# Attention blocks of four tokens, 64 moving columns instead of 128, with two buffers for keys and values

## The chip, the cores and the metric

The kernel runs on one NeuronCore of a Trainium2 chip, with float32 data throughout. The metric is the device time of one execution in microseconds (us). Five engines are named as in the profile: PE (matrix products, with PEld for its weight loads), DVE (vector), ACT (scalar and activation), POOL (GpSimd), and SP, which here does nothing but issue transfers. Transfers run on 16 DMA engines that all queues share.

## The reference, cut to what matters

There are 64 sequences of 64 tokens with 256 features. Four layers follow one another, each added to its input: a conditioned low-rank layer (0), a layer whose weights are decoded from the condition (1), an attention (2) and a set of normalised tables with a two-layer network (3). The change lies in layer 2, whose attention is unusual: it does not go over tokens. Within each token the 256 features are 16 heads of 16 numbers, and the heads attend to one another. Queries, keys and values are the same array:

```python
kx = modulated_linear(x, s, k_aff_w, k_aff_b, k_w, k_b)
kx = kx.reshape(B, N, H, D)          # H = D = 16
q = k = v = kx
scores = jnp.einsum('bnhd,bnjd->bnhj', q, k) / math.sqrt(D)
A = jax.nn.softmax(scores, axis=-1)
out = jnp.einsum('bnhj,bnjd->bnhd', A, v).reshape(B, N, F)
out = modulated_linear(out, s, o_aff_w, o_aff_b, o_w, o_b)
```

So every one of the 4096 tokens has two products of 16x16 by 16x16.

## The kernel before

**Tiling.** Layers 0, 1 and the first half of layer 2 (`layers01`) work on chunks of 512 tokens, eight in all. Attention (`fetch` and `attention`) and the rest (`layers23`) work on 16 pieces `P` of 256 tokens.

**Attention as block products.** PE contracts over 128 partitions, but a token needs only 16. The kernel puts 8 tokens (digit `b`, 8 x 16 = 128 partitions) on the partitions, and for each of 32 groups `g` of eight tokens runs one product with 128 moving columns. The moving side is block-diagonal: `kb` holds the keys of token `b` only in columns of block `b`, with zeros elsewhere, so that the eight tokens do not mix. The weight side has 32 columns, and four groups go to the four 32-column strips of the array, by the partitions of their output. A group has 16 heads as weight columns, so 16 of its 32 weight columns are zeros: `kz` holds the heads of each group between zeros, and two groups `h` = 0 and 1 add into one strip (`start=(h == 0), stop=(h == 1)`). This is L789 (`pS`), 32 products a piece, which the profile counts as 64 matmul records, two for each float32 product. L813 (`pv`) does the same with the softmax weights `at_` against the block-diagonal values `vb`, into two PSUM banks, again 32 products a piece.

**How the operands get there.** ACT writes the keys of layer 2 to `kT` (L710), PE transposes them (`pt`, L721), ACT copies them to `kk` (L727, L730). SP writes `kk` to DRAM as `kd` (L736, two transfers in 64-byte runs) and `vd` (L744, four transfers in 64-byte runs). `fetch` reads them back: `kc` (L754, one transfer), which ACT copies between the zeros of `kz` (L756); eight transfers into the blocks of `kb` (L762); eight into the blocks of `vb` (L767). There are two `kz` tiles, used in turn, and one `kb` and one `vb`, both inside the tile `kv`. After the scores DVE and ACT make the softmax (L796 to L801), DVE transposes it to `at_` (L803), PE runs L813, ACT copies both banks to `av` (L818), SP writes `av` to DRAM as `ad` (L822, 512 KB) and reads it back turned as `aT` (L829, two transfers in 256-byte runs). `layers23` then begins with `aS` (L877) and the output projection `po` (L883, L886).

**What sets the order.** Nothing is issued as written. Each piece of work is a `step` with an engine, an estimated cost, what it reads and writes and a rank. `Plan.order` lists them greedily: on each engine the step that can start first by the plan's own estimates, ties by rank, goes next. The ranks are shifted by the tables `LEAD` (by stage) and `SHIFT` (by stage and piece), and `SLACK` says how much later a step of better rank may start and still be preferred. The result is one fixed sequence per engine, and each engine waits in it in order. SP's sequence holds nearly all transfers.

Of the kernel before, what the change touches and what calls it, by code (L numbers as in the profile page):

```python
# [61 lines left out]
class Plan:  # L62
# [3 lines left out]
    LANES, ISSUE, LAND, HOP, SLACK = 8, 0.54, 2.3, 0.12, 0.0  # L66
    TABLE = 1.4

    LEAD = {"down": 946.4, "fetch": 1090.6, "gather": 1168.5, "hidden": 1056.4, "keys": 938.1, "last": 1046.3,
            "load": 934.3, "load W1": 1568.6, "load W2": 1287.4, "load decoder": 1245.0, "load first": 604.2, "load ids": 902.1,  # L70
            "load keys": 911.3, "load states": 1260.1, "load up": 753.0, "mid": 546.9, "norm": 984.7, "out": 1165.7,
            "park": 927.1, "scores": 1120.2, "set W1": 1041.3, "set decoder": 215.9, "set down": 150.6, "set k": 952.6,
            "set o": 868.6, "set states": 1178.6, "turn": 1040.2, "up": 1091.5, "values": -313.8}


    SHIFT = {"down": (121.0, 0.0, -136.0, 0.0, 45.3, 0.0, 57.2, 0.0, 669.8, 0.0, 452.8, 0.0, 448.6, 0.0, 203.0, 0.0),
            "fetch": (-21.2, -95.4, 22.4, 39.5, 73.9, 129.8, -198.4, 143.2, 60.9, 236.7, -128.9, -10.1, -60.7, 22.7, -201.3, -74.5),
            "gather": (25.1, 20.6, -52.3, 44.9, 149.5, 295.4, 273.6, -73.2, 25.2, 4.2, 71.4, 347.0, 156.9, 181.1, 284.4, 233.7),
            "hidden": (-23.7, -102.8, 100.9, 97.4, -70.1, 56.9, 93.3, -244.5, -119.8, 73.4, -11.9, 193.5, 100.1, -16.4, -8.7, 2.5),
            "keys": (-138.5, 0.0, -157.5, 0.0, 320.2, 0.0, 194.1, 0.0, 169.5, 0.0, 259.2, 0.0, 207.7, 0.0, 209.6, 0.0),  # L80
            "last": (-49.6, -146.3, 100.1, 60.6, -162.7, -187.0, 32.8, 25.1, 68.0, -10.7, 96.6, -194.4, -61.8, 407.3, 397.6, 375.4),
            "load": (0.0, 0.0, 0.0, 0.0, 311.2, 0.0, 24.7, 0.0, -364.5, 0.0, 23.9, 0.0, 66.9, 0.0, 299.3, 0.0),
            "mid": (-25.3, 0.0, -351.6, 0.0, -179.2, 0.0, -1.1, 0.0, -6.1, 0.0, 131.7, 0.0, 213.3, 0.0, 249.5, 0.0),
            "norm": (-246.5, -272.7, -139.3, -283.8, -207.2, -15.7, -104.9, 40.1, -219.1, 16.5, -133.9, -101.4, -119.9, 129.5, 13.2, -265.9),
            "out": (75.9, 13.0, -112.7, -113.3, -174.2, 11.1, 82.9, 26.4, 125.1, -118.1, 220.2, -0.8, 136.4, 254.8, -8.3, 195.2),
            "park": (-302.5, 0.0, -53.5, 0.0, -775.7, 0.0, -547.9, 0.0, -550.1, 0.0, -359.8, 0.0, -152.5, 0.0, 238.3, 0.0),
            "scores": (-82.8, 70.4, 67.7, -137.7, -106.8, -38.2, 26.9, 83.3, 98.4, 82.9, 84.9, -0.6, 136.4, 144.2, 34.2, 171.0),
            "turn": (-82.0, 10.3, -20.8, -18.4, -23.5, -0.8, 77.8, 214.9, 84.7, 115.0, -41.3, 77.4, -122.1, 45.8, 69.3, 164.8),
            "up": (-344.7, 0.0, -102.1, 0.0, -238.6, 0.0, -224.7, 0.0, -115.4, 0.0, -84.9, 0.0, -54.9, 0.0, -53.0, 0.0),
            "values": (-74.2, 53.7, -70.1, -159.6, 81.8, 307.5, -59.3, -54.8, 80.6, -145.4, -166.2, -196.3, -101.8, -85.7, -218.8, 125.5)}  # L90
# [12 lines left out]
    @staticmethod  # L103
    def keys(things):
        out = []
        for t in things:
            if isinstance(t, tuple) and isinstance(t[0], Buf):
                out.append((t[0], t[1]))
            else:
                out.append((t, None))  # L110
        return out
# [147 lines left out]
def tile_kernel(ctx: ExitStack, tc: tile.TileContext, a: dict, out: bass.AP):  # L259
# [15 lines left out]
    BUFS = {"x": 3, "xr": 3, "pw": 2, "cg": 2, "mg": 2, "ei": 2, "oh": 2, "t4": 3, "kk": 2, "kc": 1, "act": 2, "E": 2,  # L275
# [5 lines left out]
    def bank(name, tag="B"):  # L281
        return Buf(ps, tag, {"A": 2, "B": 3, "C": 2, "S": 1}[tag], [128, 512], name, turns=(tag == "A"))
# [35 lines left out]

    styleq = fixed("styleq", [128, 2, B // PB, 4, 2])
# [14 lines left out]
    kz = [fixed(f"kz{i}", [128, 32 * NG + 16]) for i in range(2)]  # L334

    kv = fixed("kv", [128, 2 * NG * 128])
    kb, vb = (kv[:, i * NG * 128 : (i + 1) * NG * 128].rearrange("p (b g j) -> p b g j", g=NG, b=8) for i in range(2))
    at_ = fixed("at", [128, 32 * NH + 16])


    def consts():
# [4 lines left out]
    step("POOL", 0.4, lambda: (nc.gpsimd.memset(neghalf, -0.5), nc.gpsimd.memset(V, 0.0), nc.gpsimd.memset(bigtab, 0.0),  # L346
                               nc.gpsimd.memset(at_[:, 32 * NH :], 0.0)),
         w=["neghalf", "V", "at0", "zeros"], rank=-107)
# [138 lines left out]
    for n, half in (("kb", 0), ("vb", 1)):  # L487
        step("POOL", 3.5, lambda half=half: nc.gpsimd.memset(kv[:, half * NG * 128 : (half + 1) * NG * 128], 0.0),
             w=[n] + [f"W_dec{i}" for i in range(NW)], rank=-104)


    for n in "ko":
# [8 lines left out]
        if n == "o":  # L501
            step("DVE", 1.0, lambda: [nc.vector.tensor_copy(
                styleq[:, k].rearrange("p c (q z) l -> p c q z l", z=2)[:, :, :, z, :], style["o"][:, k, :].rearrange("p (c l q) -> p c q l", l=2, q=2))
                for k in range(2) for z in range(2)], r=["style_o"], w=["styleq"], rank=rk)
# [117 lines left out]
    kds, vds, kcs, xds = {}, {}, {}, {}  # L622

    def layers01(c, rank):
# [66 lines left out]
        for h in range(2):  # L691
# [11 lines left out]
             r=X + ["style_k"], w=[xs], rank=rank)  # L703
        kT = sb("t4", [128, 2, CH], f"kT_{c}")
        pk = banks(f"pk_{c}")
        for o in range(2):
# [3 lines left out]
                nc.scalar.activation(kT()[:, o, b * S : (b + 1) * S], pk[o]()[:, b * S : (b + 1) * S], AF.Identity,  # L710
                                     scale=demod["k"][:, o, b0 + b : b0 + b + 1], bias=col["k_b"][:, o : o + 1])
                for b in range(CB)], r=[pk[o], "demod_k", "cols"], w=[(kT, o)], rank=rank)
        for p in range(2):
# [19 lines left out]
            kd = kds[P] = Buf(dram, "kd", 2 * NC, [HD, PT, NH], f"kd_{P}")  # L733
            vd = vds[P] = Buf(dram, "vd", 2 * NC, [8, NH, NG, HD], f"vd_{P}")
            for t in range(2):
                step("SP", 0.75, lambda t=t, kk=kk, kd=kd: nc.sync.dma_start(  # L736
                    kd()[:, t * 128 : (t + 1) * 128, :].rearrange("d p h -> p d h"),
                    kk()[:, 0, t, :].rearrange("p (d h) -> p d h", h=NH)), r=[(kk, t)], w=[(kd, t)], rank=rank + PERIOD * p, dma=(131072, 64), late=1.5)
            for cc in range(4):
                def f(cc=cc, kk=kk, vd=vd):  # L740
                    k = kk()
                    src = k[cc : cc + 1, 1]
                    src = bass.AP(src.tensor, src.offset, [[4 * k.ap[0][0], 32], [HD, 2 * NH], [1, HD]])
                    nc.sync.dma_start(vd()[2 * cc : 2 * cc + 2].rearrange("l h g d -> g (l h) d"), src)  # L744
                step("SP", 0.78, f, r=[(kk, 2)], w=[(vd, cc)], rank=rank + PERIOD * p, dma=(65536, 64), late=1.5)

    def fetch(P, rank):


        plan.stage = "fetch"  # L750
        kd, vd = kds[P], vds[P]

        kc = kcs[P] = sb("kc", [128, NG * NH], f"kc_{P}")
        step("SP", Plan.ISSUE, lambda: nc.sync.dma_start(kc(), kd().rearrange("d (b g) h -> (d b) (g h)", b=8)), r=[kd], w=[kc], rank=rank, dma=(262144, 2048))  # L754
        z = P % 2
        step("ACT", act(512), lambda: nc.scalar.copy(view(kz[z], [[32, NG], [1, NH]], 16), kc().rearrange("p (g h) -> p g h", h=NH)),  # L756
             r=[kc], w=[f"kz{z}"], rank=rank)
        for b in range(8):

            def f(b=b):  # L760
                dst = kb[b : b + 1, (b % 4) * 2 + b // 4]
                nc.sync.dma_start(bass.AP(dst.tensor, dst.offset, [[8 * dst.ap[0][0], HD], [1, NG * NH]]),  # L762
                                  kd()[:, b * NG : (b + 1) * NG, :].rearrange("d g h -> d (g h)"))
            step("SP", 0.63, f, r=[kd, "kb"], w=[f"kb.{b}"], rank=rank, dma=(32768, 2048))
        for b in range(8):

            step("SP", 0.50, lambda b=b: nc.sync.dma_start(  # L767
                vb[b * 16 : (b + 1) * 16, b].rearrange("p g d -> p (g d)"), vd()[b].rearrange("h g d -> h (g d)")),
                r=[vd, "vb"], w=[f"vb.{b}"], rank=rank, dma=(32768, 2048))

    def parts(n):
        return [f"{n}.{b}" for b in range(8)]

    aTs = {}

    def attention(P, rank):

        kzt = kz[P % 2]
        fetch(P, rank)
        plan.stage = "scores"  # L780

        pS = bank(f"pS_{P}", "S")

        def f():
            for r in range(4):
                for h in range(2):
                    for cc in range(4):
                        g = h * 16 + r * 4 + cc
# [258 lines left out]
```

## Time and profile before

| | |
|---|---|
| median of 9 runs | 487.79 us (481.22 to 494.13) |
| the profiled execution's own time | 491.37 us |
| its span, first to last instruction | 489.6 us |
| PE busy | 423.6 us (87%) |
| DVE, ACT, POOL busy | 308.7, 297.0, 155.3 us |
| mean granted TensorE clock | 0.923 |
| DMA | 192668 packets, 83.53 MB; the SP queue's packets took 50.8% of 16 engines' span |

Busy time of an engine counts the time in which at least one of its instructions ran; matmuls on different strips run side by side, so the mean of one instruction times their number is more than the busy time. The chain that ended last follows the work back from the last instruction, at each step to what released it. It is one path through an execution: taking time off it shows what can be won, and another path may then be the longer one. A DMA-issuing instruction on SP lasts as long as SP is held up by it, and counts as issue (SPq), not as busy.

### The profile page before, as it was taken

How to read it: one execution, taken by the hardware profiler on the slowest of the kernel's cores; microseconds unless marked ns; L12 is line 12 of the kernel's file. 1: busy time of each engine (PE TensorE's matmuls, PEld its weight loads, DVE VectorE, ACT ScalarE, POOL GpSimd, SP SyncE). 2: the span in 40 equal slices, each digit the busy share in tenths (PEclk: the TensorE clock that was granted, in tenths of full speed). 3: DMA queues.
4: the chain of work that ended last, by engine and by line, in shares of the span. 5: the costliest groups of instructions: out<-in, count | busy, mean ns of one | idle time of the engine just before them, and what ended most of it. 6: DMA issues, size and time to landing. Idle time of an engine off the chain costs nothing.

```text
span 489.6 us, 11060 instructions
## 1 busy us (share of the span) xinstructions
PE 423.6 (87%) x4026; PEld 321.7 (66%) x4026; DVE 308.7 (63%) x668; ACT 297.0 (61%) x875; POOL 155.3 (32%) x164
## 2 busy tenths in 40 slices
PE   4899949876869699999999989999798987999890
PEld 2886624653647377768776867788566766888770
DVE  0568894560955518677959765859683863876541
ACT  1303916529635776499549855995597964866530
POOL 5551040000243305116521660344233534256110
PEclk9957977978879889999999999999899997999997
DMA  8998577577594766857886897488777777775000
GB/s 274 304 227 269 113 140 209 130 95 177 75 179 137 234 128 176 183 152 241 169 260 109 246 180 207 105 221 153 181 173 253 136 151 215 189 214 154 23 21 21
DMA packets 192668, 83.53 MB, mean 171 GB/s; under 512 B 159819, under 2 KB 174119, under 8 KB 192615
## 3 DMA queue, kind: packets, MB, share of 16 engines
q1 hardware_dynamic: 184679, 57.81, 50.8%
q0 software_dynamic: 6656, 20.98, 15.7%
q10 hardware_dynamic: 1280, 4.05, 2.2%
q8 instruction: 32, 0.52, 0.4%
q14 instruction: 21, 0.17, 0.1%
HBM read 56.91 MB, written 25.89 MB: 169 GB/s over the span
## 4 chain that ended last, share of the span: by engine, by line
PE 52%; SPq 10%; DVE 10%; ACT 10%; DMA 8%; issue 5%; POOL 1%; another core or an unknown queue 1%; POOLq 0%; ACTq 0%; DVEq 0%
PE ph L943 15%; PE pv L813 5%; PE po L883 4%; PE pS L789 4%; PE pq L951 4%; PE pk L707 3%; PE pU L469 3%; SPq L762 3%; SPq L767 3%; ACT kT L710 2%; PE p L637 2%; DMA aT<-ad 2%; PE pz L688 2%; DMA kc<-kd 2%; ACT t L656 2%
## 5 line engine op out<-in xcount | busy, mean ns | idle before, releaser
L842 POOL TENSOR_TENSOR rs_x<-rs_x,neghalf 128x2 f32<-128x2 f32 x16 | 13.0, 811 | 118.3 <-DVE rs_x L841 117.2
L886 ACT ACTIVATE ot<-po,cols,demod_o 128x64 f32<-128x64 f32 x128 | 40.9, 426 | 11.3 <-PE po L883 11.3
L856 POOL DMA_INDIRECT mg<-in_ms_tab,ids x32 | 33.8, 1056 | 33.6 <-PE pfs L928 19.1
L710 ACT ACTIVATE kT<-pk,cols,demod_k 128x64 f32<-128x64 f32 x128 | 39.6, 442 | 7.3 <-PE pk L707 7.3
L856 POOL DMA_INDIRECT pw<-in_pw_tab,ids x32 | 35.2, 1099 | 17.7 <-PE pfh L928 10.4
L883 PE MATMUL po<-aS,w_o 128*128 128x256 f32 x128 | 32.7, 400 | 6.5 <-DVE aS L877 6.5
L813 PE MATMUL pv<-kv,at 128*32 128x128 f32 x1024 | 34.7, 283 | 4.0 <-DVE at L803 2.4
L943 PE MATMUL ph<-ft,W_t 128*128 128x256 f32 x128 | 36.5, 411 | 1.8 <-issue 1.5
L856 POOL DMA_INDIRECT cg<-in_cg_tab,ids x32 | 32.7, 1020 | 16.3 <-issue 7.8
L943 PE MATMUL ph<-fh,W_h 128*128 128x256 f32 x128 | 34.7, 396 | 3.3 <-issue 2.8
L789 PE MATMUL pS<-kv,kz 128*32 128x128 f32 x1024 | 33.6, 283 | 4.1 <-DMA kv<-vd 3.3
L707 PE MATMUL pk<-xs,w_k 128*128 128x512 f32 x64 | 33.9, 674 | 3.3 <-issue 2.3
L813 PEld LDWEIGHTS pv<-kv,at 128*32 128x32 f32 x1024 | 28.4, 113 | 11.3 <-issue 3.9
L789 PEld LDWEIGHTS pS<-kv,kz 128*32 128x32 f32 x1024 | 28.7, 114 | 9.7 <-issue 4.4
L943 PE MATMUL ph<-fs,W_s 128*128 128x256 f32 x128 | 34.9, 397 | 0.1
L842 POOL TENSOR_TENSOR rs_h<-rs_h,neghalf 128x2 f32<-128x2 f32 x16 | 13.1, 818 | 67.3 <-DVE rs_h L841 67.2
L943 PE MATMUL ph<-xr,W_x 128*128 128x256 f32 x128 | 34.1, 390 | 0.0
L656 ACT ACTIVATE t<-pu,ugT 128x64 f32<-128x64 f32 x128 | 27.5, 378 | 7.8 <-PE pu L651 3.9
L883 PEld LDWEIGHTS po<-aS,w_o 128*128 128x128 f32 x128 | 24.5, 197 | 11.6 <-issue 7.3
L951 PE MATMUL pq<-W,hs 128*128 128x256 f32 x128 | 31.9, 388 | 0.3
L943 PEld LDWEIGHTS ph<-ft,W_t 128*128 128x128 f32 x128 | 23.7, 198 | 10.8 <-issue 6.2
L946 ACT ACTIVATE hs<-ph,cols 128x256 f32<-128x256 f32 x32 | 14.9, 473 | 25.8 <-PE ph L943 24.5
(228 smaller groups left out, 954.6 us busy)
## 6 DMA issues: line engine op xcount, KB each, us to landing
ad<-av SPq DMA_DIRECT2D x16, 512.0 KB
x<-in_xT SPq DMA_DIRECT2D x8, 512.0 KB
xd<-x SPq DMA_DIRECT2D x8, 512.0 KB
xr<-xd SPq DMA_DIRECT2D x16, 256.0 KB
kd<-kk SPq DMA_DIRECT2D x32, 128.0 KB
vd<-kk SPq DMA_DIRECT2D x64, 64.0 KB
kc<-kd SPq DMA_DIRECT2D x16, 256.0 KB
kv<-kd SPq DMA_DIRECT2D x128, 32.0 KB
```

Source lines behind the costliest of these rows:

```text
L656: nc.scalar.activation(t1()[:, d, h * 256 + b * S : h * 256 + (b + 1) * S], pu[h]()[:, d * 256 + b * S : d * 256 + (b + 1) * S], AF.Copy, ...
L707: step("PE", 1.82, lambda o=o: [mm(pk[o](), wT["k"][:, k, o * 128 : (o + 1) * 128], xs()[:, k, :], start=(k == 0), stop=(k == 1)) for k in ...
L710: nc.scalar.activation(kT()[:, o, b * S : (b + 1) * S], pk[o]()[:, b * S : (b + 1) * S], AF.Identity, scale=demod["k"][:, o, b0 + b : b0 + ...
L789: mm(pS()[32 * cc : 32 * cc + 32, r * 128 : (r + 1) * 128], kzt[:, g * 32 + 16 : g * 32 + 48] if h == 0 else kzt[:, g * 32 : g * 32 + 32], ...
L813: mm(pv[h]()[32 * q : 32 * q + 32, r * 128 : (r + 1) * 128], at_[:, c0 : c0 + 32], vb[:, :, q * 8 + h * 4 + r, :], start=True, stop=True)
L842: step("POOL", 1.25, lambda: nc.gpsimd.tensor_tensor(rs(), rs(), neghalf[:, 0:2], ALU.pow), r=["neghalf"], w=[rs], rank=rank)
L856: step("POOL", 1.35, lambda dst=dst, tab=tab, i=i, t=t: nc.gpsimd.indirect_dma_start(out=dst()[:, t, :], out_offset=None, in_=a[tab], in_o ...
L883: step("PE", 1.74, lambda: [mm(po()[:, o * PT : (o + 1) * PT], wT["o"][:, k, o * 128 : (o + 1) * 128], aS()[:, k, :], start=(k == 0), stop ...
L886: step("ACT", 1.16, lambda o=o: [nc.scalar.activation(ot()[:, o, b * S : (b + 1) * S].rearrange("p (z s) -> p z s", z=2), po()[:, o * PT : ...
L943: mm(dst(), W1[n][:, k, o * 128 : (o + 1) * 128], rhs()[:, k, :], start=False, stop=(n == "h" and k == 1))
L946: step("ACT", 0.37, lambda o=o, dst=dst: nc.scalar.activation(hs()[:, o, :], dst(), AF.Silu, bias=col["int_b1"][:, o : o + 1]), r=[ph[o], ...
L951: step("PE", 0.90, lambda t=t: [mm(pq()[:, t * D : (t + 1) * D], hs()[:, k, t * 128 : (t + 1) * 128], W2[:, k, :], start=(k == 0), stop=(k ...
```

## The change

The blocks have four tokens instead of eight, so that a product has 64 moving columns instead of 128. The 128 partitions now hold two token digits, four tokens by two; the moving side is block-diagonal over the four (`kb`, `vb` as `p (b g j)` with `b=4`), and the weight side carries zeros over the digit of two: `kz` and `at_` are `[128, 32, 2, 16]`, of whose 32 weight columns 16 are non-zero on any partition. Thus no two products add into one strip any more. The number of products stays: 32 for the scores and 32 for the values of a piece, with half the moving columns. The values of a piece fill one PSUM bank instead of two.

Around it: `kz` is written by four transfers from `kd` (64-byte runs) instead of one transfer and an ACT copy; `kb` is filled by four transfers instead of eight; `kb` and `vb` exist twice, in the same `kv` tile; `kd` is written by four transfers instead of two, with the same bytes; DVE transposes the softmax in two halves; ACT copies one bank to `av`; `ad` has half its bytes and `aT` is read in runs of 128 bytes instead of 256; `kT` is written in another token order, which makes `styleq` (four small DVE copies at the start) needless; `LEAD`, `SHIFT` and `SLACK` have other values, so the sequence on each engine is another one.

```diff
-    LANES, ISSUE, LAND, HOP, SLACK = 8, 0.54, 2.3, 0.12, 0.0
+    LANES, ISSUE, LAND, HOP, SLACK = 8, 0.54, 2.3, 0.12, 0.1
...
-        return Buf(ps, tag, {"A": 2, "B": 3, "C": 2, "S": 1}[tag], [128, 512], name, turns=(tag == "A"))
+        return Buf(ps, tag, {"A": 2, "B": 3, "C": 2, "S": 1}[tag], [128, 512], name, turns=(tag in "AS"))
...
-    kz = [fixed(f"kz{i}", [128, 32 * NG + 16]) for i in range(2)]
-
-    kv = fixed("kv", [128, 2 * NG * 128])
-    kb, vb = (kv[:, i * NG * 128 : (i + 1) * NG * 128].rearrange("p (b g j) -> p b g j", g=NG, b=8) for i in range(2))
-    at_ = fixed("at", [128, 32 * NH + 16])
+    kz = [fixed(f"kz{i}", [128, NG, 2, NH]) for i in range(2)]
+    kv = fixed("kv", [128, 4 * NG * 64])
+    kb, vb = ([kv[:, i * NG * 64 : (i + 1) * NG * 64].rearrange("p (b g j) -> p b g j", g=NG, b=4) for i in (z, z + 2)] for z in range(2))
+    at_ = fixed("at", [128, NG, 2, NH])
...
             for t in range(2):
-                step("SP", 0.75, lambda t=t, kk=kk, kd=kd: nc.sync.dma_start(
-                    kd()[:, t * 128 : (t + 1) * 128, :].rearrange("d p h -> p d h"),
-                    kk()[:, 0, t, :].rearrange("p (d h) -> p d h", h=NH)), r=[(kk, t)], w=[(kd, t)], rank=rank + PERIOD * p, dma=(131072, 64), late=1.5)
+                for h in range(2):
+                    step("SP", 0.65, lambda t=t, h=h, kk=kk, kd=kd: nc.sync.dma_start(
+                        kd()[t, h].rearrange("d p h -> p d h"),
+                        kk()[h * 64 : (h + 1) * 64, 0, t, :].rearrange("p (d h) -> p d h", h=NH)), r=[(kk, t)], w=[(kd, 2 * t + h)], rank=rank + PERIOD * p, dma=(65536, 64), late=1.5)
...
-        step("SP", Plan.ISSUE, lambda: nc.sync.dma_start(kc(), kd().rearrange("d (b g) h -> (d b) (g h)", b=8)), r=[kd], w=[kc], rank=rank, dma=(262144, 2048))
-        step("ACT", act(512), lambda: nc.scalar.copy(view(kz[z], [[32, NG], [1, NH]], 16), kc().rearrange("p (g h) -> p g h", h=NH)),
-             r=[kc], w=[f"kz{z}"], rank=rank)
+        for h in range(2):
+            for t in range(2):
+                def f(h=h, t=t):
+                    dst = kz[z][64 * h + t : 64 * h + t + 1, :, h, :]
+                    nc.sync.dma_start(bass.AP(dst.tensor, dst.offset, [[2 * dst.ap[0][0], 32], [2 * NH, NG], [1, NH]]),
+                                      kd()[t, h].rearrange("d (y g) h -> (d y) g h", y=2))
+                step("SP", 0.65, f, r=[kd, f"kz{z}"], w=[f"kz{z}.{2 * h + t}"], rank=rank, dma=(65536, 64))
...
-            for r in range(4):
-                for h in range(2):
-                    for cc in range(4):
-                        g = h * 16 + r * 4 + cc
-                        mm(pS()[32 * cc : 32 * cc + 32, r * 128 : (r + 1) * 128],
-                           kzt[:, g * 32 + 16 : g * 32 + 48] if h == 0 else kzt[:, g * 32 : g * 32 + 32],
-                           kb[:, :, g, :], start=(h == 0), stop=(h == 1))
+            for g8 in range(8):
+                for cc in range(4):
+                    g = g8 * 4 + cc % 2 * 2 + cc // 2
+                    mm(pS()[32 * cc : 32 * cc + 32, g8 * 64 : (g8 + 1) * 64], kz[z][:, g].rearrange("p a h -> p (a h)"), kb[z][:, :, g, :],
+                       start=True, stop=True)
...
-        step("DVE", vec(512), lambda: nc.vector.transpose(at_[:, 0 : 32 * NH], E().rearrange("p g j -> p (g j)")), r=[E], w=["at"], rank=rank)
+        for h in range(2):
+            step("DVE", vec(512), lambda h=h: nc.vector.transpose(
+                at_[64 * h : 64 * h + 64, :, h, :], E()[64 * h : 64 * h + 64]),
+                r=[E, "at"], w=[f"at.{h}"], rank=rank)
...
-        pv = banks(f"pv_{P}", "C")
+        pv = bank(f"pv_{P}", "C")
...
-        ad = Buf(dram, "ad", 4, [128, HD, 64], f"ad_{P}")
+        ad = Buf(dram, "ad", 4, [128, HD, 32], f"ad_{P}")
```

## The prediction

> **What bounds the kernel now.** I read the page's busy times first, then the chain that ended last, the stretches, and last the work that the change touches.
>
> ```profile
> span 489.6 us, 11060 instructions
> PE 423.6 (87%) x4026; PEld 321.7 (66%) x4026; DVE 308.7 (63%) x668; ACT 297.0 (61%) x875; POOL 155.3 (32%) x164
> q1 hardware_dynamic: 184679, 57.81, 50.8%
> PE 52%; SPq 10%; DVE 10%; ACT 10%; DMA 8%; issue 5%; POOL 1%; another core or an unknown queue 1%; POOLq 0%; ACTq 0%; DVEq 0%
> L813 PE MATMUL pv<-kv,at 128*32 128x128 f32 x1024 | 34.7, 283 | 4.0 <-DVE at L803 2.4
> L789 PE MATMUL pS<-kv,kz 128*32 128x128 f32 x1024 | 33.6, 283 | 4.1 <-DMA kv<-vd 3.3
> ```
>
> PE is the busiest engine and half of the chain; the two lines that the change halves are 68.3 us of its 423.6. The chain's list by line gives pv 4.7% and pS 4.0%: 8.7% of 489.6 is 42.6 us on this path. The rest of the 68.3 us ran while something else was on it.
>
> The stretches (columns: stretch, length, then PE, PEld, DVE, ACT, POOL busy, granted clock, DMA share, GB/s) say how dense PE is:
>
> ```profile
> 190.00:250.00 60.00, 58.70 (x628) 45.14 (x625) 46.22 (x94) 40.86 (x115) 24.16 (x25) 1.00 0.79 193
> 310.00:370.00 60.00, 56.09 (x628) 43.67 (x625) 42.79 (x93) 45.98 (x134) 22.60 (x24) 0.97 0.76 177
> 80.00:437.00 357.00, 322.42 (x3445) 245.84 (x3444) 232.37 (x493) 247.48 (x721) 114.55 (x117) 0.95 0.74 175
> ```
>
> All 16 pieces' attention lies between 80 and 437 us, where PE is busy 90%, and 98% in the densest part. The second resource is not an engine of arithmetic: adding up the durations of SP's transfer instructions in the trace gives 298 us of those 357 (83%; 91% from 310 to 370). I read this as two bounds close together, PE first and SP's transfers second.
>
> **The products.** How long would a piece's scores take with 64 columns? The timeline has a near twin, L678: the same 128*32 weights with 64 moving columns, on two strips.
>
> ```profile
> 40.20 1.09 PE L678 MATMUL py<-x,U 128*32 128x64 f32 x32
> 41.22 0.43 PE L513 MATMUL pd_k<-sq_k,wsq_k 128*128 128x64 f32 x2
> ...
> 331.87 1.95 PE L789 MATMUL pS<-kv,kz 128*32 128x128 f32 x64
> 333.75 0.66 PE L928 MATMUL pft<-ident,cg 128*128 128x128 f32 x4
> ```
>
> From start to the next work, 32 records on two strips take 41.22 - 40.20 = 1.02 us, 64 on four take 333.75 - 331.87 = 1.88 us. Both are 16 rounds over the strips: 64 ns a round with 64 columns, 117 ns with 128. The new products are again 64 records on four strips, 16 rounds, with 64 columns. If four strips go as well side by side as two, 1.02 us. That is not certain, since four strips need twice the weight loads in the time. For it speaks the first stretch of the same piece:
>
> ```profile
> 331.87 0.42 PE L789 MATMUL pS<-kv,kz 128*32 128x128 f32 x8
> ```
>
> This is the timeline cut at 332.03: eight matmuls, two rounds, have begun 0.16 us after the first. A round streams for about 0.11 us, so all four first loads fit into the remaining 0.05 us: they overlap, or are shorter than 13 ns each. Bounds: 1.02 us from below; from above 1.88 us, no gain, if the 29.4 ns per record of pS (1.88/64) were a pace of issue and not of columns. I take 1.02, because py's round is the closest row. On the chain: 42.6 x (1 - 1.02/1.88) = **-19.5 us**. On PE altogether: 68.3 x 0.457 = 31.2 us.
>
> A rule against the change: the Trainium skill, "TensorE: Matmul & The Clock Gate", section "Wait — 56ns, not 53.3ns?", says that matmuls never start closer than about 25 ns, however few columns they have. By it 64 records need 1.6 us, and the chain would lose 6.3 us instead of 19.5. The eight starts in 0.16 us (20 ns apart, the loads included) do not fit it across strips; the trace has no long run on four strips with fewer columns that would decide it.
>
> **DVE's second transpose.** L803 takes 708 ns for 512 columns; the halves have 64 partitions and 512 columns each. Bounds 0 (each half as long as half) and +0.71 us a piece; I take +0.71, since columns set the time of the other DVE rows. DVE at 63% has room, but pv waits for it: PE or PEld waited for L803 five times (6.2 us). Five pieces x 0.71 = **+3.5 us**.
>
> **ACT.** It loses the copy to kz (16 x 620 ns = 9.9 us) and one of two copies to av (half of 18.8 us = 9.4 us). ACT is 61% busy, so most of it lies beside other work. Its 30.8 us of waiting before the kz copies (for kc) goes too, and frees what is queued behind it. ACT has 10% of the chain; 10% of 19.3 us is **-2 us** (bounds 0 and -19). The scattered writing of kT I cost at nothing: kk (L727), written at a stride, and ot (L886, 426 ns for 64 columns, with a rearranged write) show no charge beside kT's 442; if it cost 60 ns more per instruction (kT over t, L656, is 64), 128 of them would be 8 us of ACT.
>
> **Transfers.** Per piece, DMA packets by their mean durations in the trace: kz adds 4096 of 64 bytes, kc leaves with 128 of 2 KB (104 ns); ad's 128 fall from 4 KB (171 ns) to 2 KB; aT has 2048 of 128 bytes (13 ns, by the 120-byte ones) for 1024 of 256 (18 ns). The 64-byte ones have a pace that can be seen when kd and vd are written (window 262 to 270 us):
>
> ```profile
> GB/s 123 11 95 89 166 78 80 86 81 84 88 91 91 91 85 88 72 7 38 94 85 84 87 86 85 87 85 85 88 86 86 87 88 177 47 93 82 389 410 369
> ```
>
> It stands at 86 GB/s, 1345 packets per us, and SP is held up meanwhile (four vd issues took 4.37 us). So kz costs 4096/1345 = 3.05 us of all 16 engines; with aT +0.55, kc -0.83 and ad -0.53 it is +2.2 us a piece, 36 us altogether. DMA is 74% busy in the stretch, so most is hidden. DMA and SPq are 18% of the chain: 0.18 x 36 = **+6.5 us**. If the cover is gone, it is all 36.
>
> SP's own time: kb's eight issues become four (0.60 us each, -2.4), kc goes (-0.69), four kz come at a packet-bound 0.76 (+3.05), kd's four halves cost what its two wholes did, aT +0.3: **about +0.2 us a piece**, 0 in the sum. Lower bound per kz or kd issue: vd's median, 0.68; upper: vd's mean with its stalls, 1.09, which gives kz 4.37 and kd 4.36 for 2.1, so +3.9 a piece. Everything in SP's queue stands behind these: vd, the aT reads that DVE's aS waits for (15.2 us now), xr, and the output.
>
> The second kb and vb remove waits of SP on PE: the queue's waits show PE as releaser of L762 and L767 with 9.8 us in all. What stands in order behind would have waited in part anyway: half, **-5 us** (bounds 0 and -9.8). One PSUM bank fewer for pv relieves the pool that ph shares; no wait in the rows prices it: 0. The setup (styleq, 4 x 190 ns; memsets in four parts) and the new sequence: in the order, as many projections follow the last pv as before, so the tail of 53 us stays: 0.
>
> **Sum:** -19.5 + 3.5 - 2 + 6.5 - 5 = -16.5, taken as -17 us against 491.4 us, the profiled execution's own time (the span and 1.8 us around it): 474.4. That execution lies 0.7% over the median of the runs, 487.8, so on their scale **471 us**; the likeliest case's own range is 462 to 482.
>
> **Rivals.**
>
> *The full PE saving (chance 0.18): 455 us.* PE keeps its 90% in the stretch and loses all 31.2 us: (322.4 - 31.2)/0.903 = 322.5 for 357, -34.5, 491.4 - 34.5 = 456.9, or 454 on the runs' scale. For it: 98% PE in the densest part. Against: SP's 298 us would be 92% of it.
>
> *Products no faster, paced by issue (0.10): 490 us.* Gain 0, the other terms +3, so 494.4, or 491, less for the part that still shortens. For it: the nearly equal 32 and 29 ns a record of py and pS. Against: the eight starts.
>
> *The gain goes into another wait (0.06): 488 us.* Chain pieces on DMA aT and SPq take the place; nothing measurable.
>
> *SP's queue becomes the bound, slower (0.16): 500 us.* Its place is SP in the stretch 80 to 437; its price, the kz and kd issues with stalls like vd's. SP's highest share is 91.4%; 0.914 x 357 = 326 us of issue still fit the old length, so from +28 us, 1.75 us a piece, it decides. At +2.5 (between 0.2 and 3.9) SP needs 298 + 40 = 338, the stretch 370, +13 us: 504, or 500. For it: SP stalls of 2 to 4 us behind 64-byte writes. Against: kb's halved issues.
>
> My forecast has the remaining 0.50. **Range:** 454 to 488 leaves out half of the first rival and most of the last. Faster by over 1% (about what a measurement of this kernel can tell from no change) are the forecast but for its edge, the first rival, and some of the second: 0.70; within 1%: 0.15; slower: 0.15.
>
> **What would show it.** pS and pv with 64 columns at about 18 us busy each (31 us says the issue rival), PE near 393 us; SP's issue sum in the attention stretch near 301 us (over 326 says the last rival); ACT near 278, DVE near 320; packets near 273 thousand, DMA share above 0.8. Wrong if PE falls as said and PE's idle time grows by more than 15 us: then another bound took over.

## The result and the profile after

The changed kernel takes 524.1 us (median of 20 runs, 514.8 to 538.7), where the kernel before took 491.5 us in the runs beside it: a ratio of 1.067 [1.062, 1.071]. It is slower by 6.7%, about 32.5 us. The forecast of 471 us was wrong in sign. The profiled execution took 522.4 us. In all that follows a ratio is to the kernel before in runs beside it, with a 95% interval; each kernel has some executions that are a few per cent longer than its others, and a ratio compares the shorter ones of both.

The page of the changed kernel, first the lines that answer to those shown of before:

```profile
span 520.6 us, 11032 instructions
PE 417.5 (80%) x4026; PEld 313.2 (60%) x4026; DVE 320.8 (62%) x680; ACT 288.9 (55%) x844; POOL 153.8 (30%) x166
q1 hardware_dynamic: 264807, 53.62, 53.6%
PE 45%; SPq 15%; ACT 12%; issue 8%; DMA 8%; DVE 7%; POOL 3%; POOLq 0%; ACTq 0%; DVEq 0%
L814 PE MATMUL pv<-kv,at 128*32 128x64 f32 x1024 | 25.5, 255 | 19.8 <-DVE at L804 7.8
L790 PE MATMUL pS<-kv,kz 128*32 128x64 f32 x1024 | 21.6, 232 | 11.6 <-issue 4.0
```

SP's queue moved 4 MB less in 80 thousand packets more. The two product lines fell from 68.3 us to 47.1, yet PE as a whole only from 423.6 to 417.5, and its idle time in the span grew from 66 to 103 us. On the chain PE fell from 52% to 45% and SPq rose from 10% to 15%; its list by line names the new transfer, L758, which fills `kz`:

```profile
PE ph L940 15%; SPq L758 4%; ACT kT L706 4%; PE pq L948 4%; PE po L881 3%; PE pU L467 3%; SPq L769 2%; PE p L632 2%; PE pv L814 2%; ACT junk L832 2%; DMA kv<-vd 2%; PE pS L790 2%; ACT ot L884 2%; SPq L743 2%; SPq L764 2%
```

Where in the span is the time lost? The copies to `av` (one a piece after, two before; the columns are min, median and max ns, then the first and last start) mark the ends of the attention's pieces. First before, then after:

```profile
L818 ACT COPY av<-pv x32: 563/586/710, 90.5 to 436.5; 128x512 f32<-128x512 f32 x32
```

```profile
L818 ACT COPY av<-pv x16: 1014/1057/1176, 94.0 to 466.1; 128x512 f32<-128x512 f32 x16
```

The first comes 3.5 us later, the last 29.6 us later, and from there to the end are 54.5 us, for 53.1 before. So 26 of the 31 us are lost between the first and the last piece. The delay does not grow evenly: counted in order of time, the eighth piece's last copy comes 2 us later than before, the tenth's 37, the thirteenth's 17; the two kernels go through their work in different orders. The stretches show that all engines are thinner there (columns as in the prediction; 80 to 470 is the stretch that answers to 80 to 437 before):

```profile
80.00:470.00 390.00, 318.02 (x3446) 239.60 (x3444) 247.77 (x513) 245.98 (x712) 112.71 (x118) 0.87 0.78 152
310.00:370.00 60.00, 46.03 (x545) 36.21 (x544) 38.27 (x80) 34.89 (x101) 18.98 (x20) 0.91 0.82 155
```

PE is busy 82% of the stretch for 90% before; DMA's share rose from 0.74 to 0.78 while it moved 152 GB/s for 175. More time of the DMA engines brings fewer bytes. SP's queue, in the piece whose scores begin at 256.11 (start, duration, line, and how many issues the entry gathers):

```profile
239.34 2.80 SPq L743 DMA_DIRECT2D vd<-kk  x3
242.18 0.67 SPq L758 DMA_DIRECT2D kz<-kd  x1
242.95 0.61 SPq L821 DMA_DIRECT2D ad<-av  x1
243.61 2.13 SPq L758 DMA_DIRECT2D kz<-kd  x3
246.15 0.38 SPq L959 DMA_DIRECT2D out_x<-y  x1
246.59 1.50 SPq L764 DMA_DIRECT2D kv<-kd  x2
248.19 1.24 SPq L827 DMA_DIRECT2D aT<-ad  x2
249.47 2.46 SPq L764 DMA_DIRECT2D kv<-kd  x2
251.97 2.89 SPq L769 DMA_DIRECT2D kv<-vd  x6
```

SP does not rest: these nine entries fill 14.7 us of 15.5, without one long wait for another engine. Keys, blocks of keys, blocks of values and the output read `aT` stand one behind the other in one queue, and a piece's `kz`, `kb` and most of its `vb` issues reach from 242.18 to 254.86.

The theory that the experiments test is this: the products were no bound, and the time is lost because `kz` now comes in 65,536 packets of 64 bytes. Its rivals are that SP's longer issue alone does it, whatever the packets; that the new sequence of work (the tables) does it; and that ACT's slow copy to `av` does it.

### The profile page after: what moved, and what is told of

The parts are those of the page before. It is cut to its first block, busy times and chain, and to the rows that moved or that the text cites. A ratio compares the mean times of both kernels' runs of the same rounds, so it can differ in the third digit from the quotient of the medians.

```text
span 520.6 us, 11032 instructions
## 1 busy us (share of the span) xinstructions
PE 417.5 (80%) x4026; PEld 313.2 (60%) x4026; DVE 320.8 (62%) x680; ACT 288.9 (55%) x844; POOL 153.8 (30%) x166
## 2 busy tenths in 40 slices
DMA packets 272796, 79.34 MB, mean 152 GB/s; under 512 B 241995, under 2 KB 256295, under 8 KB 272743
## 4 chain that ended last, share of the span: by engine, by line
PE 45%; SPq 15%; ACT 12%; issue 8%; DMA 8%; DVE 7%; POOL 3%; POOLq 0%; ACTq 0%; DVEq 0%
PE ph L940 15%; SPq L758 4%; ACT kT L706 4%; PE pq L948 4%; PE po L881 3%; PE pU L467 3%; SPq L769 2%; PE p L632 2%; PE pv L814 2%; ACT junk L832 2%; DMA kv<-vd 2%; PE pS L790 2%; ACT ot L884 2%; SPq L743 2%; SPq L764 2%
## 5 line engine op out<-in xcount | busy, mean ns | idle before, releaser
L881 PE MATMUL po<-aS,w_o 128*128 128x256 f32 x128 | 37.9, 448 | 13.9 <-DVE aS L875 13.9
L814 PE MATMUL pv<-kv,at 128*32 128x64 f32 x1024 | 25.5, 255 | 19.8 <-DVE at L804 7.8
L881 PEld LDWEIGHTS po<-aS,w_o 128*128 128x128 f32 x128 | 27.9, 226 | 20.1 <-DVE aS L875 13.0
L940 PE MATMUL ph<-ft,W_t 128*128 128x256 f32 x128 | 38.4, 429 | 0.5 <-ACT ft L928 0.5
L814 PEld LDWEIGHTS pv<-kv,at 128*32 128x32 f32 x1024 | 20.8, 132 | 27.9 <-issue 18.6
L943 ACT ACTIVATE hs<-ph,cols 128x256 f32<-128x256 f32 x32 | 15.2, 480 | 40.4 <-PE ph L940 33.3
L948 PE MATMUL pq<-W,hs 128*128 128x256 f32 x128 | 35.8, 426 | 0.3
L818 ACT COPY av<-pv 128x512 f32<-128x512 f32 x16 | 17.1, 1070 | 33.0 <-PE pv L814 22.9
L940 PE MATMUL ph<-fh,W_h 128*128 128x256 f32 x128 | 32.9, 381 | 0.0
L790 PE MATMUL pS<-kv,kz 128*32 128x64 f32 x1024 | 21.6, 232 | 11.6 <-issue 4.0
L948 PEld LDWEIGHTS pq<-W,hs 128*128 128x128 f32 x128 | 26.3, 214 | 6.9 <-issue 1.5
L651 ACT ACTIVATE t<-pu,ugT 128x64 f32<-128x64 f32 x128 | 27.7, 376 | 3.9 <-DVE ugT L455 3.9
```

The source lines that it names most:

```text
L651: nc.scalar.activation(t1()[:, d, h * 256 + b * S : h * 256 + (b + 1) * S], pu[h]()[:, d * 256 + b * S : d * 256 + (b + 1) * S], AF.Copy, ...
L790: mm(pS()[32 * cc : 32 * cc + 32, g8 * 64 : (g8 + 1) * 64], kz[z][:, g].rearrange("p a h -> p (a h)"), kb[z][:, :, g, :], start=True, stop ...
L814: mm(pv()[32 * q : 32 * q + 32, g8 * 64 : (g8 + 1) * 64], at_[:, g8 * 4 + q % 2 * 2 + q // 2].rearrange("p c h -> p (c h)"), vb[z][:, :, q ...
L818: step("ACT", act(512), lambda: nc.scalar.copy(av().rearrange("p d t s -> p s t d"), pv().rearrange("p (s t d) -> p s t d", t=2, d=HD)), r ...
L881: step("PE", 1.74, lambda: [mm(po()[:, o * PT : (o + 1) * PT], wT["o"][:, k, o * 128 : (o + 1) * 128], aS()[:, k, :], start=(k == 0), stop ...
L940: mm(dst(), W1[n][:, k, o * 128 : (o + 1) * 128], rhs()[:, k, :], start=False, stop=(n == "h" and k == 1))
```

## The experiments

### Were the products a bound at all?

**Half the products in the kernel before.** Each product takes 64 of its 128 columns and writes 64; the other half is not computed, and DVE and ACT read the computed half twice. Transfers and the sequence of work stay.

```diff
-  mm(pS()[32 * cc : 32 * cc + 32, r * 128 : (r + 1) * 128], ..., kb[:, :, g, :], ...)
+  mm(pS()[32 * cc : 32 * cc + 32, r * 64 : r * 64 + 64], ..., kb[:, 0:4, g, :], ...)
   (the same for pv; the readers view the 64 columns twice, with a stride of 0)
```

> The kernel before, its sequence and transfers untouched; each of its products takes only 64 of the 128 moving columns, so half of the scores and values are not computed, and DVE and ACT read the computed half twice. PE falls by about 31 us busy at most. If products with 64 columns are worth what the prediction said and PE is what bounds the kernel, 455 to 472 us, a ratio of 0.93 to 0.96 to before. If the time saved on PE goes into other waits, or the clock falls with the thinner PE work, 480 to 490 us, a ratio of 0.98 to 1.00.

Ratio 1.000 [0.991, 1.009]. Its page and a scores block in its timeline:

```profile
PE 395.9 (83%) x4026; PEld 294.8 (62%) x4026; DVE 311.5 (65%) x668; ACT 296.2 (62%) x875; POOL 155.3 (33%) x164
PE 40%; DMA 15%; ACT 14%; SPq 13%; DVE 11%; issue 5%; POOLq 0%; POOL 0%; ACTq 0%; DVEq 0%
```

```profile
205.24 1.10 PE L789 MATMUL pS<-kv,kz 128*32 128x64 f32 x64
```

The products did become as fast as the forecast said: 1.10 us for 64 records, where 1.95 stood before. PE lost 27.7 us of busy time and the kernel gained nothing that can be measured (0.9% either way, 4 us, where 19.5 were forecast): the chain's PE share fell from 52% to 40%, and DMA, ACT and SPq took it over at the same length.

**Each product twice in the changed kernel.** The opposite edit, which gives PE back the work that the change saved and repeats values that stand there already.

```diff
-  mm(pS()[...], kz[z][:, g]..., kb[z][:, :, g, :], start=True, stop=True)
+  for _ in range(2):
+      mm(pS()[...], kz[z][:, g]..., kb[z][:, :, g, :], start=True, stop=True)
   (the same for pv)
```

> The changed kernel in its own sequence, with each product of scores and values issued twice into the same place, so that PE has about the work of before (28 us more at full clock). If PE's time lies beside transfers there, the ratio to before stays within 1.06 to 1.09. If it is on the path, 1.11 to 1.13.

Ratio 1.070 [1.061, 1.079], the changed kernel's own 1.067. 2048 more matmuls, one and a half times as many as before, cost nothing that can be measured. Its page and its stretch, to be held against the 0.87 above:

```profile
PE 426.6 (82%) x6074; PEld 331.1 (64%) x6074; DVE 320.8 (62%) x680; ACT 289.9 (56%) x844; POOL 156.1 (30%) x166
80.00:470.00 390.00, 325.08 (x5324) 256.03 (x5324) 243.44 (x506) 236.90 (x681) 113.60 (x117) 0.93 0.76 149
```

The granted clock is 0.93 with the doubled products and 0.87 without, at one length of span (520.3 and 520.6 us). So the lower clock of the changed kernel goes with thinner work on PE, and a clock of 0.93 does not bring the time back as long as the work comes with it. This run alone does not part the products from the clock: PE's busy time rose by 9 us only (417.5 to 426.6), because the higher clock paid for the rest. The halved products do part them, in the kernel before: there the clock hardly moved (0.923 and 0.924 in the profiled executions, 0.94 and 0.92 on the mean of all), and 27.7 us less of PE's time were worth nothing that can be measured.

### Were transfers a bound before?

**Long runs in the kernel before.** `kd` and `vd` are written in runs of 1 and 2 KB instead of 64 bytes, with the same number of issues and the same bytes. The elements land in other places, so only the time counts.

```diff
-  kd()[:, t * 128 : (t + 1) * 128, :].rearrange("d p h -> p d h"), kk()[:, 0, t, :].rearrange(...)
+  bass.AP(kd().tensor, kd().offset + t * 128 * D, [[D, 128], [1, D]]), kk()[:, 0, t, :]
-  vd()[2 * cc : 2 * cc + 2].rearrange("l h g d -> g (l h) d"), <src [[4 * pitch, 32], [HD, 2 * NH], [1, HD]]>
+  <vd [[2 * D, 32], [1, 2 * D]]>, <src [[4 * pitch, 32], [1, 2 * D]]>
```

> The kernel before in its own sequence; kd and vd are written with the same transfers, bytes and issues, but in runs of 1 and 2 KB instead of 64 bytes, so keys and values stand in the wrong places. If the 64-byte packets (8192 a piece, 6.1 us of the 16 engines at 1345 per us) bind the kernel before already, and PE only beside them, 445 to 465 us, a ratio of 0.92 to 0.96. If PE binds it, 475 to 487 us, 0.98 to 1.00.

Ratio 0.934 [0.925, 0.944]: 32 us less than before.

```profile
PE 418.6 (91%) x4026; PEld 323.7 (70%) x4026; DVE 309.4 (67%) x668; ACT 295.9 (64%) x875; POOL 157.2 (34%) x164
q1 hardware_dynamic: 59751, 57.81, 41.5%
```

```profile
80.00:437.00 357.00, 339.44 (x3587) 262.30 (x3588) 254.54 (x547) 266.31 (x785) 128.84 (x130) 0.98 0.63 187
```

125 thousand packets fewer, the same bytes, and PE goes to 95% of the stretch (also 95% up to 409 us, where this kernel's last copy to `av` begins). This is what the kernel before was short of: not PE, which goes from 90% to 95% as soon as it is fed, but transfers in 64-byte runs.

**The same with half the products.** Both edits above together.

> The run before this one and the halved products of half_products_in_before together. If transfers cover the products' saving, halving the products is worth something here that it was not worth with the short runs: 10 to 25 us less than long_runs_in_before, a ratio of 0.88 to 0.93. If the products' saving is lost for another reason (the sequence waits of ACT and DVE, the clock), no more than 5 us less.

Ratio 0.925 [0.917, 0.932]. Against 0.934 alone the intervals overlap: half the products bring about 1% here, 5 us, and by the ends of the intervals no more than 2.7%. That decides between neither of the two cases. So the transfers in 64-byte runs are not all that covers the products' saving; what else does (waits of other engines, or the clock, 0.965 and 0.931 in the two profiled executions) is not separated.

### Is it the packets of kz, or its issues?

**Long runs for kz.** The four transfers of a piece keep their issues and bytes, but write runs of 2 KB; the heads then stand in the wrong columns of `kz`.

```diff
-  bass.AP(dst.tensor, dst.offset, [[2 * dst.ap[0][0], 32], [2 * NH, NG], [1, NH]]), kd()[t, h].rearrange("d (y g) h -> (d y) g h", y=2)
+  bass.AP(dst.tensor, dst.offset, [[2 * dst.ap[0][0], 32], [1, NG * NH]]), kd()[t, h].rearrange("d (y g) h -> (d y) (g h)", y=2)
```

> The changed kernel in its own sequence; the four transfers that fill kz stay, with the same bytes, but write runs of 2048 bytes instead of 64 (4096 packets a piece become 128), so that heads stand in wrong columns of kz. If the 64-byte packets of kz and what queues behind them on SP made the kernel slower, the ratio to before falls from 1.067 to 0.99 to 1.02 (3.05 us x 16 pieces = 49 us of DMA time gone, most of it on the path). If the new sequence or the thinner clock did, it stays at 1.05 to 1.07.

Ratio 0.985 [0.976, 0.995]. The whole loss is gone, and 1.5% more.

```profile
DMA packets 209308, 79.34 MB, mean 161 GB/s; under 512 B 176459, under 2 KB 190759, under 8 KB 209255
q1 hardware_dynamic: 201319, 53.62, 51.6%
```

63,488 packets fewer than the changed kernel's 272,796, and not a byte or an issue fewer. From 1.067 to 0.985 is 8.1 points, 40 us. (The profiled execution of this kernel, with a span of 491.7 us, lies above the median of its runs, 478.8, so little is read from it: its packets, its sums and one wait.) The issues are as many, but not as long: with the short packets gone, SP's issue sum falls from 384 to 354 us. So this run takes away the packets' time on the DMA engines and SP's stalls behind them together. SP's issue alone does not explain it: 354 us are still more than the 347 of before, and this kernel is faster.

**kz left out.** The `dma_start` of L758 goes; the scores are computed from zeros.

> The changed kernel in its own sequence, without the four kz transfers of a piece at all (kz keeps its zeros). Against kz_long_runs it shows what their four issues on SP cost without their packets: 64 x 0.67 = 43 us of SP. If SP's issue time binds, 10 to 30 us less than kz_long_runs, a ratio of 0.93 to 0.97; if packets alone do, within 5 us of it, 0.975 to 0.99.

Ratio 0.955 [0.946, 0.964]. Without the issues and the bytes too, another 3 points, 15 us, are gained. That lies in the range given for a binding issue time, but the run takes away the transfers' bytes as well, so it does not show that the issues alone are worth it. The rest of the change (four issues of `kb` fewer, no `kc` and no copy to `kz`, second buffers, shorter products, and against them `kd`'s four transfers, the second transpose and the slow copy to `av`) is thus worth 4.5%, 22 us, if keys came for nothing. That mixes several parts, which no run here takes apart.

**kz issued by ACT.** The same packets, from ACT's queue.

```diff
-  nc.sync.dma_start(bass.AP(dst.tensor, ...   # kz
+  nc.scalar.dma_start(bass.AP(dst.tensor, ...
```

> The changed kernel in its own sequence, whole, with the four kz transfers issued from ACT's queue instead of SP's, at the same places of the order. Packets and bytes stay. If SP's place in order is what the 64-byte packets hurt (everything behind them on SP stands still), 490 to 505 us, a ratio of 1.01 to 1.04. If the 16 engines' time is (they are shared by all queues), 515 to 530 us, 1.05 to 1.09, as ACT now stands still as well.

Ratio 1.045 [1.038, 1.053], between the two ranges. SP's issue sum over the span falls from 384 us to 306, under the 347 of before. If SP's issue alone were the cause, this kernel would be no slower than before; two thirds of the loss stay. The Trainium skill, "DMA: Bandwidth & Descriptors", section "Issuing engines are not separate DMA queues", says that transfers started by different engines run on the same 16 DMA engines and that spreading them saves only the issue time, which it calls usually small. The run agrees in kind, though the issue time was not small: 2.2 of 6.7 points are won by taking it off SP. What ACT loses by issuing is not separated here; that the rest lies with the packets rests on the long runs of `kz`, which leave every issue on SP and its sum above that of before.

### Is it the sequence of work?

**Both kernels without the tables.** All entries of `LEAD` and `SHIFT` count as zero, so both are ordered by the piece alone (`SLACK` keeps its two values, 0.0 before and 0.1 after).

> The kernel before with LEAD and SHIFT taken as zero: ranks by piece alone, a neutral sequence. To be read against the next run. I expect it slower than before by 3 to 12 per cent, since the waits are no longer placed by hand.

> The changed kernel with LEAD and SHIFT taken as zero, as in the run before it. If the change itself costs time (its transfers), it is slower than the run before it by 3 to 8 per cent; if only its tables fit the chip badly, it is as fast or up to 5 per cent faster.

Ratios 1.247 [1.233, 1.260] and 1.294 [1.281, 1.307]. The tables are worth 25%, twice the most that was expected. The changed kernel is slower without them too, by 3.8%. A third kernel takes the long runs of `kz` into the changed one without tables:

> The changed kernel with LEAD and SHIFT taken as zero, as in after_no_tables, and the kz transfers in runs of 2048 bytes, as in kz_long_runs (heads stand in wrong columns). If the 64-byte packets of kz are the loss in this sequence too, 1.19 to 1.25, below before_no_tables at 1.247; if that loss belongs to the sequence of the changed kernel's tables, 1.27 to 1.30.

Ratio 1.248 [1.227, 1.270], the level of the kernel before without tables (it was expected to come out below). In an order that is fitted to neither kernel the same packets make up the whole difference, as far as intervals of 1 to 2% can tell.

**Other tables for each kernel.** `LEAD` and `SHIFT` searched anew, by the plan's own estimates.

> The kernel before, whole, with its tables searched anew in the same way. It shows how much a sequence that is as good by the plan may differ on the chip. If sequences of equal plan are equal on the chip, 0.98 to 1.01; if the old tables of before were a lucky fit, 1.02 to 1.06, and as much of the 1.067 is not the change's.

> The changed kernel, whole, with LEAD and SHIFT searched anew by the plan's own estimates, as for kz_by_copy_retabled. If part of its loss is a sequence that fits the chip badly, a ratio to before of 0.99 to 1.04; if the loss is in the transfers whatever the sequence, 1.05 to 1.08.

Ratios 1.007 [0.998, 1.016] and 1.065 [1.050, 1.081]. Other tables move neither kernel, and the difference stays. The rival falls, for kernels whose tables fit their steps.

### Is it the copy to av?

The copy writes `av` at a stride of 32 elements. Turned round, it reads PSUM at a stride and writes in a row:

```diff
-  av().rearrange("p d t s -> p s t d"), pv().rearrange("p (s t d) -> p s t d", t=2, d=HD)
+  av(), pv().rearrange("p (s t d) -> p d t s", t=2, d=HD)
```

> The changed kernel in its own sequence, whole; only the copy from PSUM to av reads at a stride and writes in one run. If the order of the write sets its time, the copy falls from 1070 to about 610 ns, 7 us of ACT; on the path some 3 us, a ratio of 1.055 to 1.067. If not, 1.067.

```profile
L818 ACT COPY av<-pv x16: 585/586/671, 91.6 to 458.3; 128x512 f32<-128x512 f32 x16
```

The copy falls from 1057 ns to 586. Ratio 1.062 [1.055, 1.068], which overlaps with 1.067 [1.062, 1.071]: at most a small part of the loss, and none that is shown.

### A whole kernel without the small packets

`kz` comes by two transfers of 2 KB runs into a `kc` tile, and two ACT copies of 64 partitions put it between the zeros; the copy to `av` is turned as above.

```diff
+  for t in range(2):  # SP: every second partition of kc, from kd()[t], runs of 2 KB
+      nc.sync.dma_start(bass.AP(dst.tensor, dst.offset, [[2 * dst.ap[0][0], 64], [1, NG * NH]]), kd()[t].rearrange("a d (y g) h -> (a d y) (g h)", y=2))
-  (the four transfers into kz)
+  for h in range(2):
+      nc.scalar.copy(kz[z][64 * h : 64 * h + 64, :, h, :], kc()[64 * h : 64 * h + 64, :].rearrange("p (g j) -> p g j", j=NH))
```

> The changed kernel, whole, with kz filled as before the change was: two transfers a piece in runs of 2048 bytes into kc, and two ACT copies of 64 partitions from there between the zeros; the copy to av reads PSUM at a stride and writes it in one run, instead of the other way round (1070 ns a copy in the changed kernel, 606 before). Same tables, but the plan gives another sequence since its steps are others. If the packets and issues of kz were the loss, it lies near kz_long_runs and kz_skipped: 470 to 485 us, a ratio of 0.96 to 1.00. If the products' layout or the sequence costs more than they give, above 1.02.

Ratio 1.097 [1.089, 1.105], a miss: slower still, though the packets are gone. The tables had been made for other steps, and two new ACT steps a piece had taken whatever place their rank gave. With tables searched for it:

> The run before this one with LEAD and SHIFT searched for this set of steps, by the plan's own estimates alone. If the sequence matters beside the transfers, 5 to 20 us less than with the old tables, a ratio of 0.93 to 0.98 and thus faster than both kernels; if the plan's estimates do not reach the chip, within 5 us of it.

Ratio 1.016 [1.011, 1.021], a miss again, as 0.93 to 0.98 was expected. The tables are worth 8 points here, where they fitted the steps no longer. Five of the 6.7 points of loss are recovered in a whole kernel; it is still not faster than before, and what keeps it 3 points above the long runs of `kz` (two issues, two ACT copies, another order) is not separated. No whole kernel of this study beats the kernel before.

## Why the prediction was wrong

**The step that failed first: the bound.** I read 90% PE in the stretch and 52% on the chain as "PE first and SP's transfers second", and priced the products at -19.5 us by their 8.7% of the chain. The size of the operation was right: in the changed kernel, too, a scores block that runs through takes about what the forecast took from py's round (1.02 us):

```profile
256.11 1.10 PE L790 MATMUL pS<-kv,kz 128*32 128x64 f32 x64 [0.39 <-DMA kv<-vd]
```

(The two lines' busy time, 47.1 us, is more than the 36 that the forecast named as its sign; in the kernel before with half the products, at a higher clock and with fewer waits inside a block, it is 38.8.) The term itself measured 0 within 4 us: half products in the kernel before give 1.000; doubled ones in the changed kernel, 1.070 for 1.067, agree. The chain is one path through one execution, and when the products got shorter, a path through DMA, ACT and SPq took over at the same length. The prediction had read from the page that a second bound was near ("two bounds close together"), and then multiplied a chain share as if there were one.

**The step that failed by size: the transfers' time on the path.** The prediction had the number of packets right (273 thousand expected, 272,796 counted). The time that SP's queue takes of the 16 engines, its share times the span, rose from 249 to 279 us: 30 of the 36 that were forecast. The forecast then hid most of that behind DMA's 74%: only 18% of the transfer time was put on the path, +6.5 us. That is the term that was mis-sized. Measured, putting `kz`'s bytes into long runs brings 40 us, while the queue's time falls by 25 (279 to 254): all of it lies on the path, and more. A share of 74% with 64-byte runs in it was no sign of room: long runs for `kd` and `vd` in the kernel before took 57 us from the queue's time (249 to 192) and 32 from the kernel's. The prediction named the price "if the cover is gone, it is all 36", and that end was the near one.

Why a microsecond of `kz`'s packets costs more than one on the path, and one of `kd`'s and `vd`'s about half, stays open. `kz` stands ahead of `kb`, `vb` and `aT` in SP's queue. No wait in the changed kernel's trace ends with the landing of `kz` itself, but DVE's wait for `aT` is 22.0 us, where it was 15.2 before and is 8.8 with the long runs. That fits a delay of what stands behind `kz`; no run tests it.

**SP's issue.** Sums over the span, in us:

| issue | before | after |
|---|---|---|
| `kd` (32, then 64) | 33.7 | 53.9 |
| `vd` (64) | 69.9 | 62.8 |
| `kb` (128, then 64) | 77.4 | 47.2 |
| `kc` (16, then 0) | 11.1 | 0 |
| `kz` (0, then 64) | 0 | 62.3 |
| `vb` (128) | 62.6 | 62.0 |
| `aT` (32) | 19.7 | 22.7 |
| all of SP | 346.6 | 384.3 |

`kz` took 0.97 us each, not 0.76; `kd`'s four took 3.4 us a piece for 2.1, where I had put no charge; `kb`'s halved issues saved 1.9, not 2.4. All of SP's issue together grew by 2.4 us a piece, not by 0.2, so past the 1.75 that the last rival gave as its point; between 80 and 470 us it is 339 us, and the prediction had named over 326 as that rival's sign. That rival ("SP's queue becomes the bound, slower") named the place and had the sign; at an assumed +2.5 it said 500 us, and 520 came of it on the same scale. What it lacked is that the packets fill the shared DMA engines also when SP does not issue them: 1.045 with `kz` on ACT's queue.

**The small terms.** DVE's second transpose is as forecast: 32 of 705 ns, DVE 320.8 us for 320 expected. DMA's share in the stretch is 0.78, where above 0.8 was expected. ACT lost less than expected (288.9 us for 278): the copies to `kz` are gone, but one copy to `av` of 1070 ns on the mean replaces two of 606, so 7.7 of the 9.4 us that it was to save never came. The forecast weighed scattered writing for `kT` alone, at nothing, which held there (449 ns for 442), and did not look at `av`. The two rows that it went by do not show a scattered write at all: `kk` (L727) and `ot` (L886) read PSUM at a stride and write in a row. The waits of SP on PE for `kb` and `vb` went from 9.8 us to 0.3, so the second buffers do what they say; what that is worth was not tried alone. The tail is as forecast (54.5 us for 53.1).

**The test that the prediction gave** was "Wrong if PE falls as said and PE's idle time grows by more than 15 us". The idle time grew by 37. PE's busy time did not fall to 393, and the clock accounts for it: 417.5 us at a mean clock of 0.868 are 362 us at the full one, 423.6 at 0.923 are 391, so the work fell by 29 us at the full clock (an estimate from busy time and mean clock), and the 31 forecast at the clock of before are the same 29.

## What to carry to other kernels

A chain share prices a stage only if nothing of nearly its length runs beside it: before a gain is multiplied by it, ask what the second-longest resource does in the same stretch. Here DMA engines at 74% with 64-byte packets among their work, and SP's issue at 83%, left no room to hide 30 us more. Price a layout change by packets as well as bytes: here 64-byte runs into the zero-padded weights cost 40 us, while halving or doubling the products they served changed nothing that could be measured. A fitted order belongs to one set of steps; an experiment that adds steps is judged only after the order has been fitted again (1.097 against 1.016).

## What the runs showed of the hardware

- Four 32-column strips of PE take 64 records of 64 moving columns in 1.10 us, 17 ns a record. The rule of about 25 ns between starts that the prediction quoted (the Trainium skill, "TensorE: Matmul & The Clock Gate", section "Wait — 56ns, not 53.3ns?") would ask for 1.6 us, by an estimate from its figure; across strips the measurement decides against it.
- The granted clock was 0.868 in the changed kernel and 0.927 with doubled products at the same span. So PE's busy time can hide work: half as many matmuls again added 9 us to it (417.5 to 426.6), but 33 us once both are multiplied by the clock (362 to 395).
- An ACT copy of 512 elements from PSUM takes 1057 ns when it writes at a stride of 128 bytes and 586 ns when it writes in a row and reads PSUM at a stride.
